# Differential attention on one core: the last sequence's softmax sums divided in two steps, reciprocals in four pieces

## The chip, the cores and the metric

The kernel runs on one core of a Trainium2 chip. The metric is the device time of one execution in microseconds (us), median of three runs. The engines are named as in the profile: PE (TensorE, matmuls), DVE (VectorE), ACT (ScalarE), POOL (GpSimd), SP (the queue that issues the transfers).

## The reference, cut to what matters

Four layers act on x (2 sequences of 1024 tokens, width 512): a gated linear recurrence, a feed-forward with ternary weights, a differential attention, and the same feed-forward again. The change lies in the attention:

```python
q = jnp.concatenate([q1, q2], axis=1)            # 32 query heads of 32
k2, v2 = jnp.repeat(k, 2, axis=1), jnp.repeat(v, 2, axis=1)
scores = where(causal, q @ k2.T / sqrt(d), -big)
p = softmax(scores)
y = p @ v2                                       # y1: the first 16 heads, y2: the others
lam = sigmoid(x @ Wlam)                          # one factor for each token and head
y = y1 - lam * y2
x = x + y.reshape(B, T, D) @ Wo
```

## The kernel before, in words

Layers one and two (up to L621) are not touched. The attention (from L628) takes the heads of a sequence b in 16 **pairs** (L679): (b, g, p, par) with g the group of heads (g < 2 for q1, else q2), two heads e per pair. There are 32 pairs, numbered 0 to 31; 0 to 15 belong to sequence 0.

Each pair has six **steps** (L1065 to L1074). In a step, `weights_step` computes the scores of two units of 128 keys against up to 512 queries (t, L866, with the maxima subtracted by L874) and their exponentials (pr, L882; the ones on the diagonal are masked by POOL, L885). `maxima_step` computes the scores of the *following* pair once more (s, L805), and DVE reduces them to row maxima (L815, L820). `weigh` multiplies the exponentials of the *previous* step with the values (y, L904). Then come the other pieces of work that the table `beside` has for this pair and step (L976, `at`). POOL splits the maxima in parts (L834 to L838), PE transposes them (mt, L845), and DVE copies them (L847).

The values carry a column of ones, so a row of y is the sum of the exponentials. When a half of the queries (512 of 1024; halves qb and e both mean this) is through, ACT copies y to ys (L921), and transfers move the weighted values into `shares` (L924) and the sums into one row of `totals[b]` (L929). Step 2 of a pair ends its first half, the step after its last ends the second.

`divide(b, e)` (L934) turns the sums of one half into factors: a reciprocal of 48x512 in place (L937), the rows of y2 times lam (L939), and a split into two parts [...] (L943, L944). There is one buffer for factors. `combine(b, c, e)` (L946) spreads the factors of one **chunk** c of 128 channels with two matmuls (r, L951), multiplies the shares on DVE (L954), and subtracts y2 on POOL (L955). Chunk 2*(g % 2) + par holds the heads of a pair, so pair 31 writes only into chunk 3. `project_out` (L962) multiplies 128 tokens of the four combined chunks with Wo (b_out, L965; each matmul is two instructions in the profile) and adds the result to x (L970).

For sequence 0, all this is done beside pair 16 and after (L1018 to L1029). For sequence 1, divide(1, 0) stands at pair 31, step 3 (L1037), two combines at step 5, and the rest behind the last pair (L1078 to L1088), where only the feed-forward follows.

What sets the order: PE's instructions are issued as the program writes them, from L1063 on (`manual_schedule`). DVE's are so only from L1080; before it, and on ACT, POOL and SP, the compiler orders instructions by its own estimate of when they are ready. y has a PSUM bank of its own (`edge`); all other products share a ring of seven banks.

## Time and profile before

| | |
|---|---|
| median of 3 runs | 2145.2 us (2144.91 to 2147.58) |
| profiled execution | 2146.65 us |
| its span, first to last instruction | 2144.9 us |
| mean granted PE clock | 0.996 |
| divide(0, 0), reciprocal | 1252.99 to 1256.3 |
| divide(1, 0), reciprocal | 1734.99 to 1738.3 |
| divide(1, 1), reciprocal | 1746.57 to 1749.9 |
| the second feed-forward's first matmul | 1774.60 |

All times in the views are us from the start of the span. A timeline row gives the start, how long the row's instructions took, engine, source line, operation, output and inputs, and how many instructions the row merges; in brackets the time that the engine had stood idle before it, and what ended that. In the list of waits a row names who waited for whom, and gives us in total, times, and the longest. In the table of stretches, each engine's busy time is followed by its number of instructions, and then come the granted PE clock, the share of the transfer engines in use, and GB/s.

### The profile page before, as it was taken

What the parts mean: (1) busy time and instruction counts of PE and PEld (TensorE: products, weight loads), DVE (VectorE), ACT (ScalarE), POOL (GpSimd) and SP (SyncE); (2) the same over time, 40 slices, a digit from 0 to 9 for tenths busy, and PEclk for the clock granted to TensorE, in tenths of its full rate; (3) what the DMA queues carried; (4) which work ended last, traced back from release to release, by engine and by line L of the source; (5) the groups of instructions that cost most, each with busy time, mean ns of one, the idle gap of its engine ahead of it and who ended that gap; (6) DMA issues with size and microseconds to landing.
All of it is one profiled execution on the core that took longest, in us unless ns stands there. A gap on an engine that the chain in (4) does not pass through costs nothing.

```text
span 2144.9 us, 28054 instructions
## 1 busy us (share of the span) xinstructions
PE 2108.8 (98%) x10615; PEld 1242.2 (58%) x10624; DVE 1069.1 (50%) x2272; ACT 835.2 (39%) x1590; POOL 449.8 (21%) x812
## 2 busy tenths in 40 slices
PE   8999999999999999999999999999999999999998
PEld 3444444688888854444444444444545447888887
DVE  5766686533343234555555465464546662433322
ACT  4444333234344322444444422243434523333333
POOL 1312212122122221111111113021212221121212
PEclk9999999999999999999999999999999999999999
DMA  6111211600000111111110101201110033000000
GB/s 255 59 59 62 86 59 74 250 1 1 1 1 1 35 46 37 41 26 41 23 44 21 46 8 37 57 20 42 24 32 15 14 111 132 20 1 20 1 20 20
DMA packets 50999, 98.71 MB, mean 46 GB/s; under 512 B 10800, under 2 KB 19120, under 8 KB 50864
## 3 DMA queue, kind: packets, MB, share of 16 engines
q1 hardware_dynamic: 50864, 96.93, 13.8%
q8 instruction: 83, 1.36, 0.3%
q14 instruction: 52, 0.43, 0.1%
HBM read 58.75 MB, written 16.78 MB: 35 GB/s over the span
## 4 chain that ended last, share of the span: by engine, by line
PE 83%; DVE 8%; DMA 4%; ACT 2%; issue 1%; POOL 1%; SPq 1%; DVEq 0%; ACTq 0%; POOLq 0%
PE y L904 12%; PE g L524 11%; PE u L524 11%; PE f_out L545 11%; PE s L805 10%; PE pq L737 8%; PE t L866 8%; PE pv L702 3%; PE b_out L965 2%; DMA w<-in_w_pt_dram 1%; DMA w_kept<-w 1%; DVE one L174 1%; PE kv L269 1%; DVE w L179 1%; PE ag L269 1%
## 5 line engine op out<-in xcount | busy, mean ns | idle before, releaser
L882 ACT ACTIVATE pr<-t 128x512 f32<-128x512 f32 (+3 forms) x768 | 314.8, 497 | 380.6 <-PE t L874 380.4
L815 DVE CUSTOM_DVE_ANT_0 s<-s,causal 128x128 f32<-128x128 f32 (+3 forms) x512 | 245.3, 510 | 126.1 <-PE s L805 117.4
L904 PE MATMUL y<-pr,val 128*64 128x512 f32 (+3 forms) x1536 | 291.6, 501 | 0.2 <-POOL pr L885 0.2
L539 POOL TENSOR_TENSOR ssq<-ssq,sq 128x512 f32<-128x512 f32 x120 | 155.9, 1299 | 603.6 <-ACT sq L538 603.6
L530 DVE TENSOR_TENSOR h<-h,u 128x512 f32<-128x512 f32 x128 | 88.0, 688 | 362.0 <-PE u L524 355.9
L524 PE MATMUL g<-xs,w 128*128 128x512 f32 x1024 | 262.4, 398 | 0.9 <-ACT xs L474 0.7
L545 PE MATMUL f_out<-w,hs 128*128 128x512 f32 x1024 | 257.7, 394 | 0.3 <-DVE hs L533 0.3
L820 DVE TENSOR_REDUCE nmax<-s 128x1 f32<-128x512 f32 x256 | 165.0, 686 | 184.4 <-PE s L805 184.3
L524 PE MATMUL u<-xs,w 128*128 128x512 f32 x1024 | 256.4, 392 | 0.0
L805 PE MATMUL s<-gr,gr 32*128 32x512 f32 (+3 forms) x1536 | 248.8, 492 | 2.6 <-DVE nmax L815 2.6
L524 PEld LDWEIGHTS u<-xs,w 128*128 128x128 f32 x1024 | 192.4, 188 | 43.5
L545 PEld LDWEIGHTS f_out<-w,hs 128*128 128x128 f32 x1024 | 191.6, 188 | 43.9 <-DVE hs L533 1.1
L524 PEld LDWEIGHTS g<-xs,w 128*128 128x128 f32 x1024 | 190.9, 189 | 44.0 <-ACT xs L474 0.9
L866 PE MATMUL t<-gr,gr 32*128 32x512 f32 (+3 forms) x1536 | 198.8, 533 | 0.0
L904 PEld LDWEIGHTS y<-pr,val 128*64 128x64 f32 x1536 | 93.5, 136 | 179.9 <-issue 105.7
L737 PE MATMUL pq<-b_xt,w_qk 128*128 128x512 f32 x384 | 176.0, 603 | 0.0
L805 PEld LDWEIGHTS s<-gr,gr 32*128 32x128 f32 x1536 | 147.6, 185 | 46.8 <-issue 14.0
L532 ACT CAST hs<-h 128x512 fp32r<-128x512 f32 x128 | 79.4, 621 | 236.6 <-DVE h L530 236.6
L885 POOL TENSOR_SCALAR_AFFINE_SELECT pr<-pr 128x256 f32<-128x256 f32 x256 | 101.3, 408 | 332.2 <-ACT pr L882 332.2
L529 ACT ACTIVATE h<-g 128x512 f32<-128x512 f32 x128 | 76.5, 598 | 224.3 <-PE g L524 224.1
L533 DVE TENSOR_TENSOR hs<-h,hs 128x512 fp32r<-128x512 f32 x128 | 88.6, 692 | 83.1 <-ACT hs L532 83.1
L737 PEld LDWEIGHTS pq<-b_xt,w_qk 128*128 128x128 f32 x384 | 69.6, 189 | 88.0 <-issue 74.0
(155 smaller groups left out, 2211.0 us busy)
## 6 DMA issues: line engine op xcount, KB each, us to landing
w<-w_kept SPq DMA_DIRECT2D x32, 768.0 KB, 8.7
w_kept<-w SPq DMA_DIRECT2D x16, 768.0 KB, 3.2
gr<-gr SPq DMA_DIRECT2D x96, 128.0 KB, 2.3
w<-in_w_gu_dram SPq DMA_DIRECT2D x32, 256.0 KB, 2.8
share<-ys SPq DMA_DIRECT2D x128, 64.0 KB, 2.0
w_in<-in_w_in_t_dram SPq DMA_DIRECT2D x5, 1024.0 KB, 11.2
x<-in_x_dram SPq DMA_DIRECT2D x16, 256.0 KB, 7.1
w<-in_w_pt_dram SPq DMA_DIRECT2D x16, 256.0 KB, 3.5
```

Of the source, the lines that this page charges most:

```text
L524: nc.tensor.matmul(po, ws[f][:, part, ts(k, P)], xs[:, e, k, :], start=(k == 0 and e == 0), stop=(k == NKC - 1 and e == 1),)
L533: nc.vector.tensor_sub(hp[:, 1, :], h, hp[:, 0, :].bitcast(F32))
L539: nc.gpsimd.tensor_add(ssq, ssq, sq)
L545: nc.tensor.matmul(po[j], hp[:, e, ts(j, P)], ws[f][:, 2, :], start=(f == 0 and e == 0), stop=(f == NF - 1 and e == 1),)
L737: nc.tensor.matmul(po, w[:, k, ts(kind, P)], xts[b][:, k, ts(e, BLK)], start=(k == 0), stop=(k == NKC - 1),)
L805: nc.tensor.matmul(part, queries[:, ts(j, P)], keys[:, first : first + nk], start=True, stop=True,)
L815: nc.vector.tensor_tensor_reduce(part, part, causal[:, BLK - part.shape[-1] :], -1.0, 3.0e38, ALU.add, ALU.min, top,)
L820: nc.vector.tensor_reduce(top, part, AX.X, ALU.max, negate=True)
L866: nc.tensor.matmul(banks[u, e][:, :nq], keys[:, ts(kb, P)], queries[:, (qb + 1) * BLK - nq : (qb + 1) * BLK], start=True, stop=False,)
L882: nc.scalar.activation(pr[:, e, :nq], banks[u, e][:, :nq], AF.Exp)
L885: nc.gpsimd.affine_select(out=pr[:, :, :P], in_=pr[:, :, :P], compare_op=ALU.is_ge, fill=0.0, base=0, pattern=[[0, 2], [1, P]], channel_mu ...
L904: nc.tensor.matmul(y[64 * e : 64 * e + 64, lo:], all_values[:, HV * (NH * kb + h) : HV * (NH * kb + h) + 64], pr[:, e, : BLK - lo], start= ...
```

## The change

The rows of pair 31 no longer go into `totals[1]`. In pair 30, step 3, POOL copies `totals[1]` into a second tile (`late`, in the slot of the attention's weights), and pair 31's sums land there. divide(1, e) runs twice for each half: once on `totals[1]`, and again on `late`, into the same single factors buffer and under the same name. divide(1, 0) moves to pair 31, step 0; combines of chunks 0 and 1 to step 3; then, still step 3, the second division; the combine of chunk 2 to step 4. Chunk 3 follows behind the last pair. The projection is cut in the same way: chunks 0 to 2 of a token tile, and chunk 3 apart. All divisions but the two on `late` take the reciprocal in four pieces of 48x128, those of sequence 0 too.

```diff
+            tot = held["late"] if pair == pairs[-1] else totals[b]
...
-                    out=totals[b][32 * (g // 2) + h : 32 * (g // 2) + h + 1, ts(qb, BLK)],
+                    out=tot[32 * (g // 2) + h : 32 * (g // 2) + h + 1, ts(qb, BLK)],
...
-        def divide(b, e):
-
-            part = totals[b][:, ts(e, BLK)]
-            nc.vector.reciprocal(part, part)
+        def divide(b, e, late=None):
+
+            part = (totals[b] if late is None else late)[:, ts(e, BLK)]
+            if late is None:
+
+                for i in range(NKC):
+                    nc.vector.reciprocal(part[:, ts(i, P)], part[:, ts(i, P)])
+            else:
+                nc.vector.reciprocal(part, part)
...
+        def late_totals(b):
+
+            sums = b_b.tile([32 + NH, SEQ], F32, tag="w_qk", name=f"late_tot{b}")
+            nc.gpsimd.tensor_copy(sums, totals[b])
+            return sums
...
-        def project_out(b, j, w_o, psum=ring_bank):
-            po = psum(f"b_out{b}_{j}")
-            for k in range(NKC):
+        outputs = {}
+
+        def project_part(b, j, w_o, chunks, psum=ring_bank):
+            if 0 in chunks:
+                outputs[b, j] = psum(f"b_out{b}_{j}")
+            po = outputs[b, j]
+            for k in chunks:
...
-            xi = xres[b * NQ + j]
-            nc.vector.tensor_add(xi, xi, po)
+            if NKC - 1 in chunks:
+                xi = xres[b * NQ + j]
+                nc.vector.tensor_add(xi, xi, po)
+
+        def project_out(b, j, w_o):
+            project_part(b, j, w_o, range(NKC))
...
-        at(n, 3, divide, 1, 0)
-        for c in range(2):
-            at(n, 5, combine, 1, c, 0)
+
+        at(n - 1, 3, lambda: hold("late", late_totals, 1))
+        at(n, 0, divide, 1, 0)
+        for c in range(NKC - 1):
+            at(n, 3 + c // 2, combine, 1, c, 0)
+        at(n, 3, lambda: divide(1, 0, held["late"]))
...
-        for c in range(2, NKC):
-            combine(1, c, 0)
         ordered.enter_context(tc.manual_schedule(engines={mybir.EngineType.DVE}))
+        late, w_o = held["late"], held["o", 1]
+        early, rest = range(NKC - 1), range(NKC - 1, NKC)
+        project_part(1, 0, w_o, early)
+        combine(1, NKC - 1, 0)
         divide(1, 1)
-        for j in range(QB - 1):
-            project_out(1, j, held["o", 1])
-        for c in range(NKC):
+        for j in (1, 2):
+            project_part(1, j, w_o, early)
+        for j in range(3):
+            project_part(1, j, w_o, rest)
+        for c in early:
             combine(1, c, 1)
-        for j in range(QB - 1, NQ):
-
-            project_out(1, j, held["o", 1], ring_bank if j < NQ - 1 else edge_bank)
+        project_out(1, QB - 1, w_o)
+        divide(1, 1, late)
+        for j in range(QB, NQ - 2):
+            project_part(1, j, w_o, early)
+        combine(1, NKC - 1, 1)
+        project_part(1, NQ - 2, w_o, early)
+        for j in range(QB, NQ - 1):
+            project_part(1, j, w_o, rest)
+
+        project_part(1, NQ - 1, w_o, range(NKC), edge_bank)
         ordered.close()
```

More of the change, by code (lines that the diff above doesn't have):

```diff
@@ L682 @@
         ]
-        groups, nmax, lams, totals, shares, factors = {}, {}, {}, {}, {}, {}
+        groups, nmax, lams, totals, shares, factors, held = {}, {}, {}, {}, {}, {}, {}
         def load_weights(b, g):
@@ L929, in weigh @@
                 nc.sync.dma_start(
-                    out=totals[b][32 * (g // 2) + h : 32 * (g // 2) + h + 1, ts(qb, BLK)],
+                    out=tot[32 * (g // 2) + h : 32 * (g // 2) + h + 1, ts(qb, BLK)],
                     in_=ys[64 * e + HD : 64 * e + HV],
                 )
-        def divide(b, e):
-            part = totals[b][:, ts(e, BLK)]
-            nc.vector.reciprocal(part, part)
+        def divide(b, e, late=None):
[5 more added lines that the diff above has]
+                nc.vector.reciprocal(part, part)
             second = part[rows_of[1]]
             nc.vector.tensor_mul(second, second, lams[b][rows_of[1], ts(e, BLK)])
-            factors[b, e] = b_c.tile([96 + NH, BLK], F32R, tag="factors", name=f"factors{b}_{e}")
+            n = f"{b}_{e}" if late is None else f"{b}_{e}_late"
+            factors[b, e] = b_c.tile([96 + NH, BLK], F32R, tag="factors", name=f"factors{n}")
             nc.gpsimd.memset(factors[b, e].bitcast(F32), 0.0)
@@ L977, in at @@
             beside.setdefault((n, step), []).append((f, args))
-        held = {}
         def hold(key, f, *args):
```

## Prediction

> **What bounds the kernel now.** First the busy shares of the page:

> ```profile
> PE 2108.8 (98%) x10615; PEld 1242.2 (58%) x10624; DVE 1069.1 (50%) x2272; ACT 835.2 (39%) x1590; POOL 449.8 (21%) x812
> ```

> TensorE (PE) is busy for 98% of the span, and the change leaves its instructions as they are in number and shape. So only PE's idle stretches and its clock can move the time. Second view: PE's waits, by line waited for.

> ```profile
> PE s L805 <- DVE nmax L815: 2.6, 1, 2.6
> ...
> PE r L951 <- DVE factors L944: 1.8, 1, 1.8
> ...
> PE b_out L965 <- POOL share L955: 0.6, 1, 0.6
> ```

> These three are the waits that the change can touch; the other large ones lie in the first layer and at the edge of the feed-forward. Third: the timeline of VectorE (DVE) around the first of them.

> ```profile
> 1251.24 0.70 DVE L815 CUSTOM_DVE_ANT_0 s<-s,causal 128x512 f32<-128x512 f32 x1 [1.65 <-PE s L805]
> ...
> 1252.99 3.35 DVE L937 RECIPROCAL tot<-tot 48x512 f32<-48x512 f32 x1 [0.99 <-DMA tot<-ys]
> 1256.27 0.40 DVE L815 CUSTOM_DVE_ANT_0 s<-s,causal 128x256 f32<-128x256 f32 x1
> ```

> This is divide(0, 0). The program has it in pair 16, step 1; it runs in pair 15, step 4, since DVE's order is the compiler's there and it takes what it believes ready. It even waits 0.99 us for the sums to land, then holds DVE for 3.35 us, and four maxima (L815) that pair 16 needs stand behind it. Fourth: PE there, and the same step one sequence later (pair 30), where no reciprocal is in the way.

> ```profile
> 1253.00 1.13 PE L866 MATMUL t<-gr,gr 32*128 32x512 f32 x8
> ...
> 1257.54 1.51 PE L805 MATMUL s<-gr,gr 32*128 32x384 f32 x8 [2.59 <-DVE nmax L815]
> 1258.98 3.44 PE L904 MATMUL y<-pr,val 128*64 128x512 f32 x8
> ...
> 1262.82 0.70 PE L866 MATMUL t<-gr,gr 32*128 32x256 f32 x8
> ```
> ```profile
> 1712.85 1.13 PE L866 MATMUL t<-gr,gr 32*128 32x512 f32 x8
> ...
> 1714.98 1.94 PE L904 MATMUL y<-pr,val 128*64 128x512 f32 x8
> ...
> 1717.18 0.70 PE L866 MATMUL t<-gr,gr 32*128 32x256 f32 x8
> ```

> From t to t it is 9.82 us against 4.33: the stall costs 5.5 us, not 2.6. Up to y it has cost 5.98 - 2.13 = 3.85; the rest is the clock, as stretches of 1 us show (the third number from the end is the granted clock):

> ```profile
> 1259.00:1260.00 1.00, 1.00 (x5) 0.41 (x6) 0.96 (x2) 0.00 (x0) 1.00 (x3) 0.63 0.00 0
> 1260.00:1261.00 1.00, 1.00 (x4) 0.24 (x2) 0.98 (x2) 0.00 (x0) 0.26 (x1) 0.50 0.00 0
> ```

> PE runs at half clock from 1259.3 to 1262.7: 3.4 us, which cost 1.65. Fifth: the end of the attention.

> ```profile
> 1737.75 0.82 PE L904 MATMUL y<-pr,val 128*64 128x384 f32 x4
> 1740.32 1.19 PE L951 MATMUL r<-factors,head_of 112*128 112x512 f32 x4 [1.75 <-DVE factors L944]
> 1741.44 0.87 PE L904 MATMUL y<-pr,val 128*64 128x256 f32 x8
> 1742.24 1.20 PE L951 MATMUL r<-factors,head_of 112*128 112x512 f32 x4
> ```
> ```profile
> 1734.99 3.35 DVE L937 RECIPROCAL tot<-tot 48x512 f32<-48x512 f32 x1 [2.74 <-DMA tot<-ys]
> ```

> PE waits 1.75 us for the factors (reciprocal 3.35, product 0.72, cast 0.42, difference 0.69, and gaps: 5.33 from 1734.99), at full clock. From 1742.24, when the last y is through, to the feed-forward's first matmul at 1774.60 there are 32.4 us. The work in them is 12 r at 0.28 (by the starts above) and 64 b_out instructions at 0.422 (40 of them from 1757.73 to 1774.60), 30.4 us; so 2.0 are small stalls.

> **Part 1, reciprocals in four pieces.** No row has a 48x128 reciprocal. L815 takes 0.30 at 128 columns and 0.73 at 512, so a fixed part of 0.16; the piece is then 0.16 + 3.19/4 = 0.96, of which some 0.1 overlaps the next: 0.87 from start to start, 3.5 us for four instead of 3.35. What counts is the order: after each piece DVE can take an L815, which is earlier in the program, as it did at 1256.27 before the rest of the division. Without the reciprocal L815 would have begun at 1251.85 (1711.70 in pair 30, less 459.85); it began 4.4 late, and PE lost 3.85, so 0.6 us is slack. With one piece ahead (DMA until 1252.99, then 0.87) it is 2.0 late and PE loses 1.4 at full clock; with two, 2.3; with three, 3.2 and the half clock again. The four L815 follow directly on the 512-wide one in pair 30, so the free slot that the compiler saw must be short: I take one piece. Gain 5.5 - 1.4 = 4.1. Bounds: 5.5 (all beside other work) and -0.2 (four in a row). divide(0, 1) ran at 1273.54 under the value matmuls, no PE wait followed it: nothing.

> [...] The row shows half clock after 2.59, while gaps of 2.06 and 2.07 (at 41.93 and 205.79) and 1.75 (at 1740.32) show none. I take the row: 4.1, and a limit between 2.1 and 2.6.

> **Part 2, the copy of the sums and the early division.** POOL's copy of 48x1024 in pair 30 lies between the memset of that shape (0.95 to 1.0) and a two-input operation (1.29 for 512 columns, so 2.6); I take 1.6, near the select's 0.41 for 256. It must await the sums of pair 30's first half (issued at 1711.12, some 1.7 to landing: 1712.9), and POOL's queue behind it holds pair 31's maxima split (L834, 1713.20, 1.4 long) and the selects (L885). The split would end at about 1716.0, before PE's mt transposes at 1716.86: nothing; with 2.6 us it costs 0.2. divide(1, 0), now in pair 31, step 0 and free to go ahead of it, adds 5.4 us to DVE between 1715 and 1733. DVE idles some 9 us there, in holes of 0.8 to 2.9, with pair 31's maxima and maxima copies behind: 0 (each piece in a hole) to 2.5 (all in a row, less holes and the slack of 0.6); as for part 1 I expect single pieces and take 0.4 in all. The memset of a further factors tile is 0.52 on POOL, beside.

> **Part 3, the wait before the last y.** Chunks 0 and 1 (four r, 1.12) move ahead of step 4's matmuls, chunk 2 (two r) behind y of step 3. But chunk 2 is traced after the second division of that half has replaced the factors, so its r need the late ones, and behind those r stand in PE's queue step 5's t, y of step 4 and the last y. PE arrives at 1736.1 + 1.2 = 1737.3. The late chain cannot start before 1734.99 (same ys copy, same DMA), and the four share products of chunks 0 and 1 (0.61 each) are earlier in the program and ready from 1733.5, so they go first or between: reciprocal from 1735.9, factors at 1741.2 to 1741.5; at 1742.8 if the reciprocal goes first and they cut into its chain. I take 1741.5: 4.2 us idle where it was 1.75. [...] the clock then halves for 3.4 us, part of which may fall in the wait: 0.6 to 2.3, I take 1.4. Last y ends at 1741.5 + two r 0.58 + t and y of step 4 (1736.10 to 1738.57) 2.47 + 0.83 = 1745.4, and 1.4 for the clock: 1746.8.

> **Part 4, the order behind it.** After the last y: 64 b_out 27.0 and ten r 2.8, 29.8. Where do stalls go? Chunk 3's r come after 2.5 us of b_out and find their factors. divide(1, 1) begins when its two products are through (4.3 after the last y), ends at 9.7; PE asks for it at 10.7: hidden, with 1.0 in hand. Then DVE has three x additions, six products and one more addition, to 16.5, and the late division runs to 21.8; PE asks at 20.9: 0.9 waiting. Chunk 3's share is subtracted by 25.0, needed at 24.95. Sums of norm statistics (L109, 0.69 each) that slip in between: 0.4. Together 31.1 where it was 32.4. The late sums hold the w_qk slot until then; reloads of feed-forward weights behind it in SP's queue are needed one per 5.6 us from 1774.6, so some 15 us later is still in time: nothing.

> Feed-forward starts at 1746.8 + 31.1 = 1777.9 instead of 1774.6: +3.3. With 1741.2 and little clock loss it is +2.2, with 1742.8 and two halved windows +5.5.

> **Sum.** -4.1 + 0.4 + 3.3 = -0.4, on a span of 2144.9: 2144.5. The profiled execution took 2146.65, 1.75 more than its span and 1.45 more than the median of 2145.2; with the same distance the median becomes 2144.8.

> **Rivals.**
> 1. Slower: the compiler's plan has long holes in DVE's work, and puts three or four pieces in a row. From three on, PE's gap at 1255 passes the limit again and nothing is won there (+0.2 for the pieces' fixed parts), the same happens to divide(1, 0) in pairs 30 and 31 (1.5, midway), and the end costs its 3.3: +5.0, 2150.2. For it: the whole 3.35 us was placed there. Against: in pair 30 the L815 follow one another without a hole.
> 2. Faster: the end doesn't wait longer, because the late chain goes ahead of the share products unbroken (1740.3) and the clock stays up, so that it costs 0.3, and the pieces all lie in holes (5.5): -4.8, 2140.4. Against: L815 cut into the division at 1256.27, and the wait is 3.0 even then.
> 3. The share products cut into the late chain (1742.8), two halved windows: +5.5 + 0.4 - 4.1 = +1.8, 2147.0.

> **Chances.** Likeliest case 0.44 (its own range 2142.8 to 2147.2), rival 1 0.24, rival 2 0.20, rival 3 0.12. Within 0.2% (4.3 us, about what a measurement of this kernel can tell from no change): the first and third but some 0.06, a third of rival 1 and a quarter of rival 2: 0.63. Slower 0.21 (0.16 of rival 1, 0.05 of that rest), faster 0.16 (0.15 of rival 2, 0.01). The range, 2140.8 to 2150.2, cuts off about half of rivals 1 and 2 each.

> **What would show it.** At about 1255: one or two reciprocals of 48x128 and then L815, a PE wait under 1.8, no halved clock. At about 1738 to 1742: PE r waiting for factors for 4 us, then half clock; chunk 2's r after the second division's difference. In the tail one wait of about 1 at the last two r. Wrong, if the pieces stand in a row, if a new PE wait appears in pairs 30 and 31 around the copy or the early pieces, or if the wait for the late factors is under 2 us.

## The result and the profile after

The changed kernel takes 2165.7 us (median of six; 2161.8 to 2170.8) where the kernel before takes 2149.2: ratio 1.0079, 95% interval 1.0059 to 1.0099, slower by some 17 us. (Before's six are the three runs given above and three more, of 2150.8 to 2152.8.) The profiled execution, the fastest of the six, took 2161.76 us with a span of 2160.0, 15.1 more than the span of before. The prediction said no change, and its range ended at 2150.2; it was wrong.

The page's first line looks as it did:

```profile
PE 2120.2 (98%) x10624; PEld 1246.1 (58%) x10624; DVE 1079.6 (50%) x2292; ACT 835.1 (39%) x1590; POOL 451.9 (21%) x815
```

PE's busy time is 11.4 us longer, though it has no other work. Its stretches of half clock come to 27.3 us where before had 10.2 (without the one at the very end, which both have). At half clock the same matmuls take longer (the eight y at 1721.23 3.68 us, 1.94 in before at 1714.98), and all that time counts as busy: half of the 17.1 us more, at most 8.5. (Before's trace also lacks the records of nine small matmuls of the first layer, which adds to the difference.) So the waits of PE show only a part of the loss (us in total, times, longest):

```profile
PE t L866 <- DVE share L967: 3.7, 1, 3.7
PE r L964 <- DVE factors_late L951: 2.7, 1, 2.7
...
PE s L805 <- DVE nmax L815: 1.6, 4, 0.7
PE t L866 <- DVE nmax L820: 1.1, 1, 1.1
```

None of these is the wait that was predicted: r did not wait for the late factors beside pair 31 (the 2.7 is in the tail). To place the 15.1 us, take the start of the same PE instruction in both traces:

| PE instruction | before | after | later by | added in between |
|---|---|---|---|---|
| t of pair 15, step 4 | 1253.00 | 1253.88 | 0.88 | 0.88 (first layer) |
| t of pair 30, step 4 | 1712.85 | 1714.98 | 2.13 | 1.25 |
| next t there | 1717.18 | 1725.36 | 8.18 | 6.05 |
| pair 31, end of step 3's y | 1732.96 | 1741.15 | 8.19 | 0.01 |
| last y through | 1742.24 | 1756.98 | 14.74 | 6.55 |
| feed-forward's first matmul | 1774.60 | 1789.68 | 15.08 | 0.34 |

The 0.88 stands ahead of everything that the change touches (after's trace has one more half-clock stretch there, from 206.4). The rest lies at three places.

**Pair 15.** DVE's timeline of after:

```profile
1253.87 0.95 DVE L941 RECIPROCAL tot<-tot 48x128 f32<-48x128 f32 x1 [1.00 <-DMA tot<-ys]
1254.74 0.40 DVE L815 CUSTOM_DVE_ANT_0 s<-s,causal 128x256 f32<-128x256 f32 x1
...
1256.21 2.56 DVE L941 RECIPROCAL tot<-tot 48x128 f32<-48x128 f32 x3
...
1259.98 0.69 DVE L951 TENSOR_TENSOR factors<-tot,factors 48x512 fp32r<-48x512 f32 x1
1260.69 0.69 DVE L820 TENSOR_REDUCE nmax<-s 128x1 f32<-128x512 f32 x1
```

One piece, then the four maxima, as predicted. But then three pieces, the product with lam, the cast and the difference go in a row, 4.48 us from 1256.21 to 1260.69, ahead of the next maximum (L820). PE of after:

```profile
1253.88 1.13 PE L866 MATMUL t<-gr,gr 32*128 32x512 f32 x8
...
1256.02 1.51 PE L805 MATMUL s<-gr,gr 32*128 32x384 f32 x8 [0.19 <-DVE nmax L815]
...
1259.65 0.70 PE L866 MATMUL t<-gr,gr 32*128 32x256 f32 x6
1261.44 0.37 PE L866 MATMUL t<-gr,gr 32*128 32x128 f32 x1 [1.08 <-DVE nmax L820]
...
1262.36 2.36 PE L805 MATMUL s<-gr,gr 32*128 32x512 f32 x6 [0.38 <-DVE nmax L815]
```

From t to t it is 5.77 us where it was 9.82. One step further, PE waits 1.08 and 0.38, and the granted clock is halved from 1264.5 to 1267.9 (0.50 in the stretch from 1265 to 1266). By 1310 PE is 1.74 later than before, 0.86 more than ahead of the step. (Another 0.37 is lost near 1397, in e1 below too; its cause was not looked for.)

**Pair 30.** DVE of after, and the copy on POOL that it waits for:

```profile
1716.28 0.94 DVE L941 RECIPROCAL tot<-tot 48x128 f32<-48x128 f32 x1 [1.93 <-POOL late_tot L956]
...
1719.05 1.75 DVE L941 RECIPROCAL tot<-tot 48x128 f32<-48x128 f32 x2
...
1722.71 0.69 DVE L820 TENSOR_REDUCE nmax<-s 128x1 f32<-128x512 f32 x1
```
```profile
1715.22 1.03 POOL L956 COPY late_tot<-tot 48x1024 f32<-48x1024 f32 x1 [9.18 <-DMA tot<-ys]
```

The early division, written for pair 31, step 0, has gone ahead into pair 30, step 4, in front of three maxima that PE is about to need. There it also waits 1.93 us for the copy, because it changes in place the sums that POOL still reads. PE's waits of 0.74 and 0.24 for maxima (L815) follow, and the clock is halved from 1718.5 to 1725.3. DVE's next maximum (L820) begins 7.73 us after the step's t; before had it 1.98 after (1714.83), so DVE is 5.75 us late there, and PE loses 6.05.

**Pair 31.** DVE of after:

```profile
1743.14 3.35 DVE L943 RECIPROCAL late_tot<-late_tot 48x512 f32<-48x512 f32 x1 [2.69 <-DMA late_tot<-ys]
1746.41 2.40 DVE L967 TENSOR_TENSOR share<-share,r 128x512 f32<-128x512 f32 x4
...
1749.63 1.31 DVE L950 CAST factors_late<-late_tot 48x512 fp32r<-48x512 f32 x1
1750.97 0.78 DVE L951 TENSOR_TENSOR factors_late<-late_tot,factors_late 48x512 fp32r<-48x512 f32 x1
```

PE of after:

```profile
1741.15 1.20 PE L964 MATMUL r<-factors,head_of 112*128 112x512 f32 x4
...
1747.08 1.00 PE L866 MATMUL t<-gr,gr 32*128 32x384 f32 x1 [3.68 <-DVE share L967]
...
1752.59 0.73 PE L964 MATMUL r<-factors_late,head_of 112*128 112x512 f32 x2
...
1756.98 2.84 PE L982 MATMUL b_out<-w_o,share 128*128 128x512 f32 x6
```

The late reciprocal stands in DVE's queue ahead of the four products that read r. The four r hold four of the ring's seven banks until those products have run, so the fourth t of step 4 has no bank: 3.68 us. When PE comes to chunk 2's r, the late factors are just there.

### The profile page after: what moved, and what is told of

Its sections match the earlier page's. It is cut to its first block, busy times and chain, and to the rows that moved or that the text cites. A ratio compares the mean times of both kernels' runs of the same rounds, so it can differ in the third digit from the quotient of the medians.

```text
span 2160.0 us, 28094 instructions
## 1 busy us (share of the span) xinstructions
PE 2120.2 (98%) x10624; PEld 1246.1 (58%) x10624; DVE 1079.6 (50%) x2292; ACT 835.1 (39%) x1590; POOL 451.9 (21%) x815
## 4 chain that ended last, share of the span: by engine, by line
PE 82%; DVE 9%; DMA 4%; ACT 2%; POOL 1%; issue 1%; SPq 1%; DVEq 0%; ACTq 0%; POOLq 0%
PE y L904 12%; PE g L524 11%; PE u L524 11%; PE f_out L545 11%; PE s L805 10%; PE pq L737 8%; PE t L866 8%; PE pv L702 3%; PE b_out L982 2%; DMA w<-in_w_pt_dram 2%; DMA w_kept<-w 2%; DVE one L174 1%; PE a_out L421 1%; DVE w L179 1%; ACT mag L157 1%
## 5 line engine op out<-in xcount | busy, mean ns | idle before, releaser
L815 DVE CUSTOM_DVE_ANT_0 s<-s,causal 128x128 f32<-128x128 f32 (+3 forms) x512 | 245.2, 510 | 126.0 <-PE s L805 117.4
L904 PE MATMUL y<-pr,val 128*64 128x512 f32 (+3 forms) x1536 | 295.2, 506 | 0.7 <-POOL pr L885 0.5
L820 DVE TENSOR_REDUCE nmax<-s 128x1 f32<-128x512 f32 x256 | 165.0, 686 | 185.1 <-PE s L805 185.0
L805 PE MATMUL s<-gr,gr 32*128 32x512 f32 (+3 forms) x1536 | 253.3, 493 | 1.6 <-DVE nmax L815 1.6
L866 PE MATMUL t<-gr,gr 32*128 32x512 f32 (+3 forms) x1536 | 201.0, 534 | 4.8 <-DVE share L967 3.7
L904 PEld LDWEIGHTS y<-pr,val 128*64 128x64 f32 x1536 | 94.2, 137 | 182.5 <-issue 109.0
L805 PEld LDWEIGHTS s<-gr,gr 32*128 32x128 f32 x1536 | 149.2, 185 | 48.8 <-issue 14.6
L885 POOL TENSOR_SCALAR_AFFINE_SELECT pr<-pr 128x256 f32<-128x256 f32 x256 | 101.4, 409 | 327.9 <-ACT pr L882 327.9
L866 PEld LDWEIGHTS t<-gr,gr 32*128 32x128 f32 x1536 | 67.9, 183 | 93.6 <-issue 53.5
```

What stands on the lines that cost most here:

```text
L805: nc.tensor.matmul(part, queries[:, ts(j, P)], keys[:, first : first + nk], start=True, stop=True,)
L815: nc.vector.tensor_tensor_reduce(part, part, causal[:, BLK - part.shape[-1] :], -1.0, 3.0e38, ALU.add, ALU.min, top,)
L820: nc.vector.tensor_reduce(top, part, AX.X, ALU.max, negate=True)
L866: nc.tensor.matmul(banks[u, e][:, :nq], keys[:, ts(kb, P)], queries[:, (qb + 1) * BLK - nq : (qb + 1) * BLK], start=True, stop=False,)
L885: nc.gpsimd.affine_select(out=pr[:, :, :P], in_=pr[:, :, :P], compare_op=ALU.is_ge, fill=0.0, base=0, pattern=[[0, 2], [1, P]], channel_mu ...
L904: nc.tensor.matmul(y[64 * e : 64 * e + 64, lo:], all_values[:, HV * (NH * kb + h) : HV * (NH * kb + h) + 64], pr[:, e, : BLK - lo], start= ...
```

## The experiments

All were timed against the kernel before on the same chip. Line numbers are those of each kernel. `behind(ins, f)` gives what f adds a fixed place in its engine's queue: after the instruction ins. `held` keeps such instructions by name.

**e1_pieces: the pieces alone.** The kernel before, and only this:

```diff
-            nc.vector.reciprocal(part, part)
+            for i in range(NKC):
+                nc.vector.reciprocal(part[:, ts(i, P)], part[:, ts(i, P)])
```

> The kernel before with only the reciprocals of all divisions in four pieces. Theory (place in DVE's queue): after the first piece the four maxima go, but the other three pieces, the product, the cast and the difference stand ahead of the next maxima, so PE's gap only moves one step on and the half clock comes again: from +0 to +2 us against before, the stretch from pair 15 step 4 to pair 16 as long as before (within 1.5 us). Rival (the prediction's step): the pieces give 4 us back, ratio 0.998, and all of the slowdown of the full change comes from the last pairs.

Measured: 2148.75 us, ratio 1.0007 (1.0000 to 1.0014), as the theory has it and not the rival. PE in pair 15:

```profile
1258.02 1.51 PE L805 MATMUL s<-gr,gr 32*128 32x384 f32 x8 [0.18 <-DVE nmax L815]
...
1263.45 0.37 PE L866 MATMUL t<-gr,gr 32*128 32x128 f32 x1 [1.09 <-DVE nmax L820]
```

The pattern of after, alone: 0.18, then 1.09, and half clock from 1266.1. The 4.1 us of the prediction's Part 1 are in the first row and gone in the second.

**e2_behind_values: the whole division, behind a copy of the values.** The kernel before; the reciprocal stays whole, but divide(0, 0) is queued on DVE behind pair 16's first copy of the values:

```diff
+            if b and j == 0:
+                held["first"] = copied.ins
...
-                    at(n + 1, 1, divide, b, 0)
+                    at(n + 1, 1, lambda b=b: behind(held["first"], divide, b, 0))
```

> The kernel before with divide(0, 0), whole, queued on DVE behind pair 16's first copy of the values, where PE has 27 us of value matmuls. Theory: no maxima stand behind it, the wait of 2.6 us and the half clock of 3.4 us at 1257 go away: -5.5 us, ratio 0.9974, no granted clock of 0.5 between 1250 and 1270. Rival (DVE's work is only moved, and the value copies or the factors of sequence 0 come late instead): 0, with a new wait between 1270 and 1310.

Measured: 2142.09 us, ratio 0.9976 (0.9968 to 0.9985). PE from t to t:

```profile
1253.95 1.13 PE L870 MATMUL t<-gr,gr 32*128 32x512 f32 x8
...
1258.28 0.70 PE L870 MATMUL t<-gr,gr 32*128 32x256 f32 x8
```

4.33 us, no wait, no half clock there. In the trace PE gains 5.4 us from before this step to the last r (0.95 later becomes 4.49 earlier), the upper bound of Part 1 (5.5). What counts was the division's place, not its pieces: behind the values' copy, DVE has time.

**e3_early_behind_turn: the early division behind pair 31's last turned maxima.** The changed kernel, with

```diff
-        at(n, 0, divide, 1, 0)
+        at(n, 2, lambda: behind(held["turn"], divide, 1, 0))
```

> The changed kernel with divide(1, 0) traced at step 2 of pair 31 and queued on DVE behind pair 31's last copy of the turned maxima; the copy of the sums on POOL stays where it was. Theory: the 6 us lost in pair 30 step 4 (DVE waits 1.9 for the copy and then runs the division ahead of the maxima, and the clock halves) go away: -6 us against the changed kernel, ratio to before about 1.005. Rival (the copy on POOL, with the maxima split behind it, is what costs there): pair 30 keeps at least 3 us of its loss, ratio about 1.007.

Measured: 2157.57 us, ratio 1.0055 (1.0043 to 1.0068); its span is 5.5 us shorter than that of the changed kernel. POOL, then PE, in pair 30:

```profile
1715.38 1.03 POOL L956 COPY late_tot<-tot 48x1024 f32<-48x1024 f32 x1 [9.17 <-DMA tot<-ys]
```
```profile
1715.14 1.13 PE L866 MATMUL t<-gr,gr 32*128 32x512 f32 x8
...
1719.48 0.70 PE L866 MATMUL t<-gr,gr 32*128 32x256 f32 x8
```

The same copy at the same place, and 4.34 us from t to t where before had 4.33. So POOL's copy by itself costs nothing, and the 6.05 belong to the division's place. In pair 31 the moved division costs a new wait of 0.95 (L127's tiles for the feed-forward).

**e4_late_behind_products: the late division behind the four products.** The changed kernel, with

```diff
-        at(n, 3, lambda: divide(1, 0, held["late"]))
+        at(n, 3, lambda: behind(held["product"], divide, 1, 0, held["late"]))
```

> The changed kernel with the late division of the first half queued on DVE behind the share products of chunks 0 and 1. Theory (PSUM banks): the four r of these chunks hold four of the seven ring banks until their products are done, and the products stand behind the late reciprocal and its wait for the sums (2.7 + 3.4 us), so step 4's fourth t waits 3.7 us; with the products first this wait is gone, PE waits later for the late factors of chunk 2 instead (4 to 5 us, half clock): 2 to 4 us less than the changed kernel. Rival (the late factors alone bound that stretch, as the prediction had it): the stretch from step 4's t to the last y keeps its length within 1 us.

Measured: 2162.45 us, ratio 1.0081 (1.0068 to 1.0093). PE beside pair 31:

```profile
1740.38 1.13 PE L866 MATMUL t<-gr,gr 32*128 32x512 f32 x8
...
1747.63 1.19 PE L964 MATMUL r<-factors_late,head_of 112*128 112x512 f32 x2 [4.04 <-DVE factors_late L951]
...
1754.38 1.98 PE L982 MATMUL b_out<-w_o,share 128*128 128x512 f32 x4
```

All eight t go through without a wait for a bank. In its place stands the wait that had been predicted, 4.04 us for the late factors (4.2 in Part 3). From the four r to the end of the last y it is 15.12 us where the change has 15.83: only 0.7 won, so the theory's 2 to 4 did not come. The factors did come earlier, 8.2 us after the first r began instead of 10.6. But half clock of 6.8 us follows the wait (the two r take 1.19 us, 0.73 in the change), and what stands behind the factors, up to the last y's end, takes 6.75 us where the change has 4.39.

This trace shows one thing more. In pair 30 it has the change's early division at the same place in DVE's queue, and PE waits 0.74 and 0.44 for L815, but no half clock follows:

```profile
1718.79 1.94 PE L904 MATMUL y<-pr,val 128*64 128x512 f32 x8
```

That y took 3.68 us in the changed kernel's trace. Yet from step 4's t of pair 30 to the end of pair 31's step 3 this run loses 5.67 us against before, and the changed kernel 6.06. By these two traces half clock is worth some 0.4 of the loss in pair 30; the rest is the division's place.

**e5_zero_matmuls: PE kept busy in that wait.** The changed kernel with 14 matmuls of zero weights into y's bank ahead of the blocked t. They add nothing to y, and nothing is left out:

```diff
+            for _ in range(14):
+                nc.tensor.matmul(
+                    outs[pair][0:64], causal[:, 0:64], causal, start=False, stop=False
+                )
```

> The changed kernel with 14 more matmuls of zero weights (bf16, 128x512) at the end of pair 31's step 3; they add nothing to y, in whose bank they accumulate, and take some 3 us just where PE waits 3.7 us for a ring bank afterwards. Theory (the half clock has a price of its own there: 6.8 us halved, of which some 1.7 lie in the wait): PE stays busy, the clock stays up, and the kernel is 2 to 3 us faster than the changed one, although it does more. Rival (the wait is all that counts, or zero weights don't keep the clock up): within 1 us of the changed one, or slower.

Measured: 2164.82 us, ratio 1.0080 (1.0066 to 1.0094). PE:

```profile
1743.37 3.21 PE L1002 MATMUL y<-causal 128*64 128x512 bf16 x14
...
1748.29 0.58 PE L866 MATMUL t<-gr,gr 32*128 32x384 f32 x1 [0.66 <-DVE share L967]
...
1753.10 0.70 PE L964 MATMUL r<-factors_late,head_of 112*128 112x512 f32 x2 [1.87 <-DVE factors_late L951]
```

The rival held. The clock stayed up through step 4's t and y (1.00 in every stretch from 1743 to 1754), and PE then waited 1.87 us for the late factors, which came no earlier (10.7 us after the first r, 10.6 in the change). So half clock ahead of the factors was no loss of its own: DVE's chain was later. But after that wait the clock was halved from 1754.6 to 1758.0, under the last y, where the change has full clock. From the four r (1742.24) to the last y's end (1758.47) it is 16.23 us, no less than the 15.83 of the change.

**e6_three_behind: all three divisions by hand.** The edits of e2, e3 and e4 together, on the changed kernel.

> The changed kernel with three divisions queued on DVE behind other work, all else kept: divide(0, 0) behind the first value copy, divide(1, 0) behind the last turned maxima, the late division of the first half behind the share products. If the places in DVE's queue are the cause, the sum closes: -5.5 at pair 15, 0 to +1 in pairs 30 and 31, and what is left is the end, +5.8 up to the last y and +0.3 behind it: +1 to +2 us against before, ratio 1.0005 to 1.001. Rival (the added division work itself, 2 x 5.3 us of DVE and two memsets and a copy on POOL, costs wherever it stands): ratio above 1.003.

Measured: 2147.53 us, ratio 1.0000 (0.9991 to 1.0008). The only long waits left beside pair 31 and behind it:

```profile
1735.93 0.70 PE L968 MATMUL r<-factors_late,head_of 112*128 112x512 f32 x2 [4.04 <-DVE factors_late L955]
...
1765.02 1.22 PE L968 MATMUL r<-factors_late,head_of 112*128 112x512 f32 x2 [2.71 <-DVE factors_late L955]
```

With every instruction of the change still there, three places in a queue take back the whole loss of 0.79%. What is left in the trace: 5.5 gained in pair 15, 1.0 lost at L127's tiles, 4.4 before the last y's end (1727.55 to 1741.25 is 13.70, where before had 9.28), 3.1 behind it (half clock of 6.8 us after the second wait; 35.5 us to the feed-forward instead of 32.4). Together that is 3.1 later; 0.9 was gained in the first layers, which nothing here touches, so the span is 2.2 longer. The gain in pair 15 comes from a place alone and can be had without the change (e2, 0.9976). Against that, the divisions in two steps still cost some 0.24%, 5 us.

**e9_zero_pair15: what is half clock worth in pair 15?** The kernel before with ten such zero matmuls in PE's gap of 2.59 us; nothing is left out.

```diff
+                if pair == pairs[16] and (step, x) == (4, 1):
+                    for _ in range(10):
+                        nc.tensor.matmul(
+                            outs[pairs[15]][0:64], causal[:, 0:64], causal, start=False, stop=False
+                        )
```

> The kernel before, with ten matmuls of 512 columns and zero weights (they add nothing to y, and no computation is left out) in the place where PE waits 2.59 us for the maxima at 1254.95, about 2.3 us of them. Nothing on VectorE moves: the delay of the maxima by the reciprocal stays. Theory of the prediction (of the 5.5 us lost in that step, 1.65 are the half clock, and it comes from PE's gap): no half clock behind it, the step takes 8.1 to 8.3 us from t to t where it took 9.82, and the time falls by 1.65: ratio 0.9992. Rival (the clock halves there for another reason): the half clock stays, 9.8 us, ratio 1.000.

Measured: 2148.53 us, ratio 0.9999 (0.9991 to 1.0007). PE:

```profile
1252.74 1.13 PE L871 MATMUL t<-gr,gr 32*128 32x512 f32 x8
...
1254.61 2.35 PE L803 MATMUL y<-causal 128*64 128x512 bf16 x10
1257.26 1.51 PE L810 MATMUL s<-gr,gr 32*128 32x384 f32 x8 [0.30 <-DVE nmax L820]
...
1260.90 0.70 PE L871 MATMUL t<-gr,gr 32*128 32x256 f32 x8
...
1739.56 1.20 PE L956 MATMUL r<-factors,head_of 112*128 112x512 f32 x4 [1.79 <-DVE factors L949]
```

From t to t it is 8.16 us, as expected, with no half clock: from the s to the next t it is 3.64, where before had 5.28. And yet the times show no gain, though their interval does not exclude the 0.9992. By the next y (1263.65, where before has 1264.45) the lead has shrunk from 1.65 us to 0.53 (PE stood 0.27 earlier than before ahead of this step), because the division has made DVE late by then, and a weight load of PE waits 0.6 for L820. The rest went at the end of the attention, where the wait for the factors (last row) was this time followed by half clock. In the table of stretches the third number from the end is the clock:

```profile
1742.00:1743.00 1.00, 1.00 (x3) 0.81 (x4) 0.97 (x2) 0.98 (x2) 0.74 (x1) 0.50 0.00 0
```

The theory of the gap held for the step; in the trace little of it is left for the time.

**e7_best: can late factors be had without the wait?** From e6: the late factors get a buffer of their own, so that chunks 0 to 2 use the early ones in steps 3 to 5; the late division stands behind chunk 0's products; the tail asks for chunk 3 last.

```diff
-            factors[b, e] = b_c.tile([96 + NH, BLK], F32R, tag="factors", name=f"factors{n}")
+            if late is None:
+                made = b_c.tile([96 + NH, BLK], F32R, tag="factors", name=f"factors{b}_{e}")
+            else:
+                made = b_p.tile([96 + NH, BLK], F32R, tag="group2", name=f"factors{b}_{e}_late", bufs=2)
...
-            at(n, 3 + c // 2, combine, 1, c, 0)
+            at(n, 3 + c, combine, 1, c, 0)
```

> A version of the change meant to beat both: as e6, but the late factors have a buffer of their own, chunks 0 to 2 use the early factors and stand at steps 3, 4 and 5 (two ring banks each), the late division is queued behind chunk 0's products, the last feed-forward input tile moves to step 3, and the last two r stand behind three partial projections. Theory: no wait for late factors before the last y and none for a ring bank, no half clock at the end; -5.5 at pair 15 and -3 to -4 at the end: ratio 0.9955 to 0.9965. Rival (the end is bound by the sums' landing and the division in any order): -5.5 alone, ratio 0.9975.

Measured: 2142.54 us, ratio 0.9980 (0.9972 to 0.9988): the rival's value, not the theory's. In the trace the end of the attention gains nothing: 7.4 us earlier than before at pair 30, and at the feed-forward too. No wait for factors, only 0.2 us for a bank and no half clock is left there, but this wait is new:

```profile
1736.71 0.44 PE L908 MATMUL y<-pr,val 128*64 128x128 f32 x4 [2.06 <-POOL pr L889]
```

On POOL, the subtraction of chunk 1's share (1.27 us from 1735.03) had gone ahead of the last mask of the exponentials (1736.25). Once more it was a place in a queue, now on POOL.

**e8_best_selects: that subtraction behind the last mask.**

```diff
+            if not late:
+                nc.gpsimd.tensor_sub(y1, y1, y2)
...
+        for c in (1, 2):
+            at(n, 5, lambda c=c: behind(held["select"], subtract, 1, c, 0))
```

> The kernel of the run before (late factors in a buffer of their own, chunks 0 to 2 on early factors, the three divisions queued by hand), and on POOL the subtractions of chunks 1 and 2 are queued behind the last select, where chunk 1's stood ahead of it and PE waited 2.06 us before the last y. Theory (that select bound the end of the attention): the wait falls to 0.5 or less and 1.5 to 3 us go: ratio 0.9965 to 0.9972. Rival (the stretch is bound elsewhere by then, and the shares or b_out wait in its place): ratio stays at 0.998.

Measured: 2141.17 us, ratio 0.9964 (0.9951 to 0.9978), faster than both kernels. PE, from the last y on:

```profile
1738.20 0.87 PE L908 MATMUL y<-pr,val 128*64 128x256 f32 x8
...
1740.56 1.13 PE L995 MATMUL b_out<-w_o,share 128*128 128x512 f32 x2 [0.44 <-POOL share L981]
```

The wait ahead of the last y is gone; b_out waits 0.44 and then 0.56 for the subtractions instead. In the trace the end of the attention gains 0.8 us against before (3.16 earlier in pair 30, 3.94 at the feed-forward). Nearly all that e8 wins is pair 15, as in e2. The intervals of e2 and e8 overlap, as do those of e7 and e8; what the late sums are worth in themselves stays at about 1 us by the trace, and isn't shown by the times.

## Why the prediction was wrong

The sum of the forecast was -0.4 us; the two traces differ by 15.1. The step that failed in Parts 1 and 2 is the same, and it is the largest part of the error: the pieces of a division were taken to fall singly into DVE's holes. In the runs most of each division stood in a row ahead of maxima that PE needed (4.48 us in pair 15), and the early division ran two steps before its place in the program, waiting for POOL's copy. With the places of three divisions fixed by hand the whole loss is gone (e6).

**What bounds the kernel** held: only PE's idle stretches and its clock moved the time.

**Part 1 (a gain of 4.1 predicted, a loss of 0.9 measured).** "One piece ahead" was right: a piece took 0.95 (0.96 predicted), t to t fell by 4.05. The step that failed is the end of the sum: it stopped at the next t and never asked where the other three pieces and the 1.9 us of product, cast and difference would go. They went in one row ahead of the next maximum, and the loss came back one step later (e1). The same goes for splitting the old stall into 3.85 and 1.65 for the clock: e9 took the clock's part away and by the next y only 0.5 of it stayed won, since DVE was late behind it. There the two costs cover each other; they don't add.

**The clock's limit ("between 2.1 and 2.6 us") fell.** e9's wait of 1.79 us at 1739.56 was followed by half clock. In the kernel before, the same wait (1.75) was not, nor was one of 2.06 in the first layer. Before's own trace had a case against the limit that the prediction left out; half clock followed this row, from 399.1 to 402.5:

```profile
397.29 0.63 PE L136 MATMUL xnt_f<-ident,xn_f 128*128 128x128 f32 x4 [1.95 <-DVE xn_f L127]
```

So the gap's length alone doesn't decide in these runs: half clock followed waits of 1.79 and 1.95 us and did not follow waits of 1.75 and 2.06.

**Part 2 (0.4 predicted, 6.05 measured)** is the largest error. POOL's copy was costed on POOL's queue, 1.6 us (1.03 measured), and rightly cost nothing there (e3). Missing was the DVE instruction that waits for it: the early division overwrites what the copy reads. "As for part 1 I expect single pieces" carried an assumption over instead of looking at pair 30's queue. The bound of 2.5 took DVE's holes between 1715 and 1733 off the division's 5.4 us. But the division went ahead of them all: in that step before had one hole of 1.17 us, and DVE came to L820 5.75 us late. Half clock of 6.8 us stands in the same place, but e4 loses 5.67 there without it.

**Part 3 (4.6 predicted, 6.55 measured)** named the right limit. The late factors came at 1751.75, 10.6 us after the end of step 3's y (1741.15); predicted were 8.5 (1741.5 less 1732.96). The step that failed is the order of reciprocal and products: the sum took "first or between", and the products went after the reciprocal and into its chain (the case of 1742.8, that is 9.8). The rest is the cast, 1.31 us instead of 0.42; while it ran (from 1749.63), POOL was subtracting shares (two, 2.95 us from 1747.70). Why it took longer is not shown. The bank that four unread r hold was not foreseen, but it comes from the same order. With the order that the prediction assumed, the factors came after 8.2 us in e4 and e6, and the stretch lost 4.4 in e6 (half clock of 3.4 us, as predicted) and 5.8 in e4 (6.8 us of it).

**Part 4 (-1.3 predicted, +0.34 measured).** The late division of the second half began 16.55 us after the last y (16.5 predicted), PE asked for it at 21.06 (20.9 predicted). It came 23.7 after the last y and not 21.8: between its reciprocal and its difference DVE did norm statistics, which nobody was waiting for yet. DVE of after:

```profile
1776.83 0.65 DVE L109 BATCH_NORM_STATS2 st_f<-x 128x6 f32<-128x512 f32 x1
1777.51 0.68 DVE L945 TENSOR_TENSOR late_tot<-late_tot,lam 16x512 f32<-16x512 f32 x1
...
1780.00 0.68 DVE L951 TENSOR_TENSOR factors_late<-late_tot,factors_late 48x512 fp32r<-48x512 f32 x1
```

The sum had 0.4 for such intrusions; three of these statistics took 1.96, so PE waited 2.70 and not 0.9.

**The rivals.** The first, the slower one, had the mechanism, though not its sizes: pieces in a row (one step later than it had them), nothing won in pair 15, the same in pair 30, the end on top. Against its terms the trace has 1.25 instead of 0.2 for pair 15 and what follows it, 6.05 instead of 1.5 for pair 30, and 6.9 instead of 3.3 for the end; with the 0.88 of the first layer these make its 5.0 the measured 15.1. What spoke against it, maxima without a hole between them in pair 30, was read from a step in which no division was in the queue.

## What to carry to other kernels

When an instruction is moved into an engine whose order the compiler chooses, its cost is everything that stands behind it in that queue, up to the first instruction that another engine waits for (in pair 30 DVE was 5.75 us late and PE lost 6.05); follow it until the engine has caught up, one step further than the first gap. Splitting a long instruction gives no protection if the pieces may be queued back to back: fixing its place behind a harmless instruction won 5 us (e2, ratio 0.9976) where four pieces won nothing (e1, 1.0007). And when one wait is removed, look for the wait just behind it before counting the gain. In these runs half clock cost time where PE's own work came last (behind the late factors it took 6.75 us in e4 and 5.32 in e6 to the last y's end, 4.39 in the change), and next to none where DVE was later still (0.4 us in pair 30; ahead of the factors in e5 nothing, they came 10.7 us after the first r, 10.6 in the change).

## What the runs showed of the hardware

```profile
205.79 1.12 PE L280 MATMUL pss<-sq,headmean 128*128 128x512 f32 x2 [2.07 <-ACT sq L289]
```
```profile
205.68 1.12 PE L280 MATMUL pss<-sq,headmean 128*128 128x512 f32 x2 [2.18 <-ACT sq L289]
```

What decides between the two is not shown.
- With useless matmuls in PE's wait there was no half clock at that place: in e5 the clock was 1.00 from 1743 to 1754, where the change had 0.50 from 1745.8 to 1752.6; in e9 the step took 8.16 us instead of 9.82. It won little (ratios 1.0080 and 0.9999): another chain was late behind them, and half clock came after a later wait instead (1.87 us in e5, 1.79 in e9).
- A reciprocal of 48x512 takes 3.35 us and one of 48x128 0.95, 0.87 from its start to that of the next instruction: four pieces in a row come to some 3.5 us, so they cost next to nothing in themselves.
